# Batch norm constants, joins, third logits and a variance placed elsewhere in the first blocks of a codebook convolution

## The chip, the cores and the metric

One Trainium2 chip; the kernel runs on one of its cores. The time is the device time of one execution in microseconds. Before the change it is 2612.57 us, the median of three runs (2611.66 to 2615.24).

Engine names in the rows of the profile: PE is TensorE's matmul and PEld its weight load, DVE is VectorE, ACT is ScalarE, POOL is GpSimd, SP is SyncE, which issues most of the transfers here. A trailing q (SPq) is the issuing queue. L614 is line 614 of the kernel.

## The reference, cut to what matters

Two convolutions of 3x3, each computed with a codebook of 16 centroids per channel, around a group norm, two batch norms, a squeeze-and-excite gate and two residual additions. Input `x` is 16 x 256 x 28 x 28, float32.

```python
def amm_conv3x3(x, centroids, w_sub):          # centroids: C x 16 x 9
    p = patches of x                           # B x 784 x C x 9
    d = sum(p*p)[..., None] - 2 * einsum('bncs,cks->bnck', p, centroids) + sum(centroids*centroids)
    attn = softmax(-d, axis=-1)                # over the 16 centroids
    lut = einsum('cks,cso->cko', centroids, w_sub)
    return einsum('bnck,cko->bno', attn, lut)

def bn(x, gamma, beta, mean, var):
    inv = gamma * rsqrt(var + 1e-5)
    return x * inv + (beta - mean * inv)

g = group_norm(x, 32 groups)
h = relu(bn(amm_conv3x3(g, centroids1, wsub1), bn1))
y = bn(amm_conv3x3(h, centroids2, wsub2), bn2)
y = y * sigmoid(relu(mean(y) @ w1 + b1) @ w2 + b2)
out = x + relu(y + g)
```

## The kernel before

The work is cut into 128 blocks: two layers, 16 images, and in each image four blocks, one for each half of the channels (`hh`) and of the rows (`t`), in the order of `BLOCKS`: (0,0), (0,1), (1,1), (1,0). A block works on 128 channels and 14 x 28 = 392 positions. Its steps are:

- **Patches.** Each of the two patch tiles `pt` holds nine shifted copies of the input. For image 0 they come straight from a prepared input (`raw`, L269 to L273), with GpSimd or Vector adding the group norm's border terms (`border`, L510 to L530). From image 1 on, the normalised image is written to memory twice (`to_home1`) and read back by six transfers (`patches`, L585 to L595).
- **Logits** (`logits`, L605 to L619): four groups `mm` = 0 to 3, each of 16 small matmuls into two PSUM banks of two halves. ScalarE takes the exponentials (`exps`, L622 to L626).
- **Denominators** (`num_b`, L673 to L684) from all four exponentials, into one double bank `nb`. ScalarE copies it twice with different masks (`split_r`, L687 to L689, and `split_q`, L697 to L699); Vector adds the other half to each (`join_r`, L691 to L695, and `join_q`, L702 to L704), takes the reciprocal (`recip_dve`, L706) and spreads it over the channels by shuffles (`spread`, L715 to L723).
- **Numerators** (`num_a`, L659 to L669), four double banks `na`; each is multiplied by the reciprocal on Vector (`scale_a`, L737 to L741) or copied by ScalarE and multiplied on GpSimd (`copy_a`, `scale_q`).
- **Products** (`product`, L745 to L752): 128x128 matmuls with the lookup table. Four blocks need only seven products for two row halves and two channel halves each, since GpSimd forms differences of the blocks' inputs (`mix`, L754 to L758) and Vector adds results (`acc_add`, L783 to L790).

For image 0 the group norm is not applied to the image but folded into the weights: `raw_stats`, `raw_mean`, `raw_dev`, `raw_var`, `raw_norm` find mean and deviation, `mean_off` (L384 to L392) subtracts a mean from the weights, `tap_sum` (a matmul, L394), `tap_scale` and `tap_shift` (L401 to L411) scale them into `wx`. All this is done for each half of the weights (`h` = 0, 1; half 0 serves the logits 0 and 1, half 1 the logits 2 and 3). `later` and `later_tap` do the same for the second channel half. The statistics of image 1 (`gn_stats`, `gn_mean`, `gn_var`, `gn_apply`, L419 to L576) are taken in the usual way during blocks 2 and 3.

**What sets the order.** Each engine does its instructions in the order in which the program issues them. That order is written by hand: `at(cl, sub, f, ...)` files a job under a step `cl` and a position `sub`, and at the end the jobs run in the order of these two keys (L1541 to L1543), jobs with equal keys in the order in which they were filed. A block takes two steps. `TURN` moves a few logits of the first blocks to other keys.

**PSUM.** There are four double banks, numbered 0 to 3, and everything uses them in turn. In the first four blocks `EARLY` says which logits, numerators, denominators, product and small matmul takes which number; a matmul that wants a bank waits until its last reader has finished. `("lg", 1): ((1, 2), ...)` means that block 1's logits 0 take bank 1 for their first half and bank 2 for the second.

**Constants.** `vecs` holds the batch norms' parameters. `setup_bn` (L319 to L324) files two inverse square roots of `var` on GpSimd at (6, 2.75); `setup_shift` (L326 to L332) files the sign change of a bias (L327) and six small products and differences on Vector at (9, 2.1).

Of the kernel before, what the change touches and what calls it, by code (L numbers as in the profile page):

```python
# [30 lines left out]
BN_EPS = 1e-5  # L31
# [21 lines left out]
EARLY = {  # L53
# [4 lines left out]
    "acc": {4: 0, 6: 1, 7: 3}, "small": {4: 1},  # L58
}
TURN = {(2, 2): (4, 0.9), (2, 3): (4, 1.035), (3, 0): (5, 1.27), (3, 1): (5, 1.32), (3, 2): (7, 1.3), (3, 3): (7, 1.35)}  # L60
LAST = {0: (12, 2.05), 1: (8, 2.05), 2: (10, 2.05), 3: (11, 2.9)}
# [27 lines left out]
def kernel(  # L89
# [219 lines left out]
    def rsqrt(dst, src, eps, n):  # L309
        t = small.tile([P, n], F32, name="rs_t")  # L310
        nc.gpsimd.tensor_scalar(t, src, eps, None, op0=ALU.add)
        nc.gpsimd.tensor_tensor(dst, t, mhalf[:, :n], ALU.pow)
# [5 lines left out]

    def setup_bn():  # L319
        for l in range(2):  # L320
            sc = const.tile([P, NB], F32, name=f"bnsc{l}")
            sh = const.tile([P, NB], F32, name=f"bnsh{l}")
            rsqrt(sc, vecs[:, :, 4 * l + 3], BN_EPS, NB)
            bn.append((sc, sh))  # L324

    def setup_shift():  # L326
        nc.vector.tensor_scalar_mul(nb2_sb, vecs[:, :, 8], -1.0)  # L327
        for l, (sc, sh) in enumerate(bn):
            ga, be, mu = (vecs[:, :, 4 * l + i] for i in range(3))
            nc.vector.tensor_mul(sc, sc, ga)  # L330
            nc.vector.tensor_mul(sh, mu, sc)
            nc.vector.tensor_sub(sh, be, sh)  # L332

    cst = const.tile([P, 64], F32, name="cst")
# [145 lines left out]
    def raw_scales(ps):  # L480
        rr, rstd = raws["rr", 0], nrm[:, 0, 1, 0:1]
        nc.gpsimd.tensor_scalar(rr[:, 0], hot_sb[:, :16], rstd, None, op0=ALU.mult)
        nc.tensor.matmul(ps[:, 16:32], lhsT=eighth, rhs=rr[:, 0], start=True, stop=True)
        sq_add(0, 1)
        scm, ms = piece(16), piece(16)
        nc.vector.tensor_scalar(scm, ps[:, 16:32], hot_sb[:, 26:27], hot_sb[:, 27:28], op0=ALU.mult, op1=ALU.add)
        nc.vector.tensor_tensor(ms, ps[:, 16:32], raws["m2", 0], ALU.mult)
        raws["scm", 0], raws["ms", 0] = scm, ms
# [762 lines left out]
    for j, u in enumerate(blocks):  # L1251
# [26 lines left out]
        at(g, 1.05, split_r, u)  # L1278
        at(g, 1.2, join_r, u)
        at(g, 1.25, recip_dve, u)  # L1280
        at(g, 1.3 if j > 1 else 1.06, split_q, u)
        at(g, 1.35 if j > 1 else 1.21, join_q, u)
        g = 2 * j + 2 + (j > 1)
        for i, mm in enumerate(SLOT_MM):
            at(g, 1.0 + 0.01 * i, num_a, u, mm)
            if mm in kept:
                at(g, 1.05, copy_a, u, mm)
            else:
                if j == 1:
                    at(4, 0.835 if i else 0.815, spread, u, mm)  # L1290
                else:
                    at(g - 1, 2.05 if i == 4 - len(kept) and j > 1 else 1.4 + 0.01 * i, spread, u, mm)
                at(g, 1.04 + 0.001 * i, scale_a, u, mm)
# [7 lines left out]
    for l in range(2):  # L1301
        for b in range(B):
# [75 lines left out]
            if l == 0:  # L1378
# [8 lines left out]
                if b + 1 < B:  # L1387
                    at(*((g - 2 + (b == 1), 2.6 - (b == 1)) if b else (1, 1.6)), load_x, b + 1)
                    for q in range(NB):
                        at(*(((g + 1, 1.5) if b == 1 else (g, 0.3)) if b else (3, 1.3)), gn_stats, b + 1, q)  # L1390
                    at(*((g + 1, 2.1) if b else (4, 0.825)), gn_mean, b + 1, step=g + 1 if b else 4)
                    at(*((g + 3, 2.1) if b else (4, 0.845)), gn_var, b + 1, step=g + 3 if b else 4)
                    for q in range(NB):
                        at(*((g + 4, 1.9) if b else (4, (0.95, 1.055)[q])), gn_apply, b + 1, q)
                        at(*((g + 4, 1.92) if b else (4 + 3 * q, 1.6 + 0.05 * q)), to_home1, b + 1, q)
            else:
# [33 lines left out]
    for o in range(2):  # L1430
        at(11 + o, 0.5 if o else 1.9, code_spread, o)
    at(8, 0.6, code_load)
    at(14, 0.7, rank_row)
# [62 lines left out]
    raw_scales(ps)  # L1496
    tap_sum(0, 0, bank("tap", tag=0)[:, :256])
    tap_scale(0, 0)
    tap_shift(0, 0)
    at(-0.4, 0.5, mean_off, 0, 256, 512)  # L1500
    at(-0.4, 0.55, tap_scale, 0, 1)
    at(0, 0.15, lambda: tap_sum(0, 1, bank("tap", tag=3)[:, :256]))
    at(0, 0.2, tap_shift, 0, 1)
    for t in xpads:
# [27 lines left out]
    at(1, 1.44, tap_scale, 1, 0, 16, nc.gpsimd)  # L1532
    at(3, 0.9, later_tap)
    for h in range(2):
        at(3, 0.91, tap_shift, 1, h)
    at(6, 2.75, setup_bn)
    at(9, 2.1, setup_shift)
    for t in hpads:
# [184 lines left out]
```

## Time and profile before

| | us |
|---|---|
| median of three runs | 2612.57 (2611.66 to 2615.24) |
| the profiled execution | 2611.61 |
| its span, first to last instruction | 2610.1 |
| TensorE busy | 2589.5 (99%) |
| Vector busy | 1778.1 (68%) |
| ScalarE busy | 1372.3 (53%) |
| GpSimd busy | 1905.7 (73%) |
| mean clock granted to TensorE | 0.999 |

A busy time counts an engine from the start of an instruction to its end; matmuls are pipelined, so a TensorE that is busy isn't always at its peak. In a row of the timeline stand the start, the duration, the engine, the line, the operation, what it writes and reads, and the count; in brackets the engine's idle time ahead of it and what ended that. In a row of waits stand who waited, for whom, the sum of the waits, their number and the longest. In a row of windows stand the stretch, its length, each engine's busy time with its count of instructions, the clock granted to TensorE as a share of the full one, and what the transfer engines did.

### The profile page before, as it was taken

The page shows a single profiled execution, that of the slowest core. Times are in us where ns is not written, and L with a number is a line of the kernel's source. Part 1 is how long each engine was busy: PE and PEld are TensorE (multiplying, and loading weights), DVE is VectorE, ACT ScalarE, POOL GpSimd, SP SyncE. Part 2 cuts the span into 40 slices and gives each one's busy share as a digit, 9 for nine tenths or more (in the row PEclk, how much of TensorE's full clock was granted, in tenths as well). Part 3 has the DMA queues.
Part 4 walks back from the last instruction along what each step waited for, and adds up shares of the span by engine and source line. Part 5 has one row for each costly group of instructions (what it writes and reads, how often), then busy time and mean ns, then how long its engine had stood idle before and what let it go on. Part 6 is the DMA issues. An engine that isn't in the chain of part 4 may idle for free.

```text
span 2610.1 us, 85834 instructions
## 1 busy us (share of the span) xinstructions
PE 2589.5 (99%) x37026; PEld 1269.1 (49%) x37026; DVE 1778.1 (68%) x3797; ACT 1372.3 (53%) x1913; POOL 1905.7 (73%) x1341
## 2 busy tenths in 40 slices
PE   8999999999999999999999999999999999999999
PEld 3444444444444444444444444444444444444445
DVE  7776656666566666566676766767776667767676
ACT  6444444444444454444455655565555655555565
POOL 6786666866568766677666887778878788787786
PEclk9999999999999999999999999999999999999999
DMA  6556656555555576554664344444444444444432
GB/s 217 147 150 183 202 155 186 165 169 167 159 145 146 167 185 178 168 159 137 180 170 105 104 118 122 124 115 119 104 128 125 119 116 110 115 126 127 116 105 66
DMA packets 213289, 372.07 MB, mean 143 GB/s; under 512 B 29497, under 2 KB 183529, under 8 KB 212329
## 3 DMA queue, kind: packets, MB, share of 16 engines
q1 hardware_dynamic: 206584, 333.75, 46.9%
q0 software_dynamic: 6176, 32.66, 3.5%
q8 instruction: 295, 4.83, 0.8%
q14 instruction: 90, 0.73, 0.1%
q10 hardware_dynamic: 144, 0.10, 0.0%
HBM read 288.46 MB, written 77.95 MB: 140 GB/s over the span
## 4 chain that ended last, share of the span: by engine, by line
PE 98%; DVE 1%; ACT 0%; POOL 0%; issue 0%; DMA 0%; SPq 0%; POOLq 0%; ACTq 0%
PE acc L749 52%; PE lg L614 17%; PE na L665 14%; PE nb L679 14%; ACT e L625 0%; PE sep L1050 0%; DVE rb L722 0%; POOL qp L758 0%; PE tap L395 0%; PE sep L1042 0%; DVE nb_sb L327 0%; DMA xt<-in_x 0%; PE sqp L377 0%; PE sqp L346 0%; POOL qp L730 0%
## 5 line engine op out<-in xcount | busy, mean ns | idle before, releaser
L749 PE MATMUL acc<-qp,wall 128*128 128x392 f32 (+1 forms) x3088 | 1099.3, 499 | 0.3 <-POOL qp L758 0.2
L625 ACT ACTIVATE e<-lg 128x784 f32<-128x784 f32 x960 | 737.8, 821 | 637.2 <-PE lg L614 634.2
L758 POOL TENSOR_TENSOR qp<-qp,qp 128x784 f32<-128x784 f32 x512 | 944.6, 1869 | 151.3 <-DVE qp L741 150.8
L749 PEld LDWEIGHTS acc<-qp,wall 128*128 128x128 f32 x3088 | 568.0, 190 | 505.9 <-issue 54.6
L722 DVE STREAM_SHUFFLE rb<-r 128x392 f32<-128x392 f32 x1024 | 550.8, 604 | 0.0
L614 PE MATMUL lg<-pt,wd 32*32 32x392 f32 x15872 | 468.9, 499 | 2.9 <-DVE hpad L786 2.0
L693 DVE SCALAR_TENSOR_TENSOR r<-nb,kst,r 128x392 f32<-128x392 f32 x128 | 80.1, 626 | 444.7 <-ACT r L689 442.3
L665 PE MATMUL na<-e,cwa 64*32 64x392 f32 x8192 | 374.5, 492 | 1.4 <-DVE gn_var L562 1.4
L741 DVE TENSOR_TENSOR qp<-na,rb 128x784 f32<-128x784 f32 x352 | 333.9, 972 | 60.8 <-PE na L665 49.8
L679 PE MATMUL nb<-e,cwb 64*32 64x392 f32 x8192 | 373.8, 492 | 0.1
L730 POOL TENSOR_TENSOR qo<-qo,rb 128x392 f32<-128x392 f32 x128 | 131.3, 1026 | 295.3 <-DVE rb L718 294.6
L707 DVE RECIPROCAL r<-r 128x392 f32<-128x392 f32 x128 | 333.2, 2603 | 4.4
L730 POOL TENSOR_TENSOR qp<-qp,rb 128x784 f32<-128x784 f32 x160 | 295.7, 1858 | 2.9
L679 PEld LDWEIGHTS nb<-e,cwb 64*32 64x32 f32 x8192 | 189.0, 106 | 175.5 <-issue 21.8
L665 PEld LDWEIGHTS na<-e,cwa 64*32 64x32 f32 x8192 | 182.0, 106 | 184.9 <-issue 75.1
L614 PEld LDWEIGHTS lg<-pt,wd 32*32 32x32 f32 x15872 | 116.1, 103 | 269.6 <-issue 235.5
L749 PE MATMUL acc<-qp,w_A 128*128 128x392 f32 x512 | 182.4, 499 | 0.0
L689 ACT ACTIVATE r<-nb,kst 128x392 f32<-128x392 f32 x128 | 86.8, 678 | 165.9 <-PE nb L679 162.8
L649 POOL TENSOR_TENSOR z<-z,mx 128x1568 f32<-128x1568 f32 x32 | 91.8, 2869 | 94.6 <-DVE mx L643 94.6
L749 PE MATMUL acc<-qo,wall 128*128 128x392 f32 (+1 forms) x386 | 157.9, 491 | 0.0
L735 ACT COPY qp<-na 128x784 f32<-128x784 f32 x160 | 130.0, 813 | 22.4 <-PE na L665 20.6
L749 PEld LDWEIGHTS acc<-qp,w_A 128*128 128x128 f32 x512 | 94.6, 190 | 82.5 <-DVE qp L741 19.8
(241 smaller groups left out, 1707.3 us busy)
## 6 DMA issues: line engine op xcount, KB each, us to landing
pt<-home SPq DMA_DIRECT2D x744, 209.0 KB
pt<-home SPq DMA_DIRECT2D x744, 104.5 KB
home<-xpad SPq DMA_DIRECT2D x30, 899.0 KB
xt<-in_x SPq DMA_DIRECT2D x30, 784.0 KB
out_dram<-y SPq DMA_DIRECT2D x31, 392.0 KB
pt<-in_p SPq DMA_DIRECT2D x6, 784.0 KB
d_wS<-st SPq DMA_DIRECT2D x12, 192.0 KB
wall<-d_wS SPq DMA_DIRECT2D x4, 576.0 KB
```

The lines of the kernel that those rows point to most:

```text
L614: nc.tensor.matmul(bk[32 * c : 32 * c + 32, :N].rearrange("p (r w) -> p r w", w=W), lhsT=(wx[u["hh"]] if early(u) else wts["wd", u["hh"]]) ...
L625: nc.scalar.activation(eg[:, 2 * i : 2 * i + 2, :], bk[:, :, :N], AF.Exp, scale=2.0)
L649: nc.gpsimd.tensor_tensor(zk, zk, mx.unsqueeze(2).to_broadcast([P, N // 4, K]), ALU.subtract)
L665: nc.tensor.matmul(bs[32 * i : 32 * i + 32, r, :N], lhsT=wts["cwa", u["hh"]][64 * r : 64 * r + 64, mm, i, :], rhs=es[64 * r : 64 * r + 64, ...
L679: nc.tensor.matmul(bs[32 * i : 32 * i + 32, r, :N], lhsT=wts["cwb", u["hh"]][64 * r : 64 * r + 64, mm, i, :], rhs=es[64 * r : 64 * r + 64, ...
L707: nc.vector.reciprocal(u["r"], u["r"])
L722: nc.vector.stream_shuffle(rb[:, r, :], u["r"], mask_of(2 * mm + r))
L730: nc.gpsimd.tensor_tensor(q, q, u.pop(("rb", mm)), ALU.mult)
L735: nc.scalar.copy(pair(u, mm), u.pop(("na", mm))[:, :, :N])
L741: nc.vector.tensor_mul(pair(u, mm), u.pop(("na", mm))[:, :, :N], rb)
L749: nc.tensor.matmul(accs[key][:, : cols[1] - cols[0]], lhsT=wl[w][:, k, :], rhs=us["q", k][:, cols[0] : cols[1]], start=first and n == 0, s ...
L758: nc.gpsimd.tensor_tensor(pair(out_u, mm), pair(in0, mm), pair(in1, mm), ALU.subtract)
```

## The change

In the order of the diff:

- block 0's numerators, and some logits of blocks 1 and 2, get other PSUM banks; block 1's third logits (`mm` = 2) move from step 3 to (2, 0.9), ahead of block 0's numerators at (2, 1.0);
- `setup_shift` is merged into `setup_bn`, and the whole moves to (1, 0.47), behind the second half's squares on Vector;
- the scale and shift of image 0's group norm (`scm`, `ms`) become a function of their own, `raw_scm`; the second half's `mean_off` moves ahead of it, and its tap sum ahead of the first logits, its tap scale and shift to (-0.4, 0.5) and (-0.4, 0.6);
- for blocks 0 and 1, `join_r` moves from 1.2 to 1.055, right behind `split_r`; `split_q` and `join_q` move into the next step, (g + 1, 0.12) and 0.13; block 0's first spreads move behind them, to (2, 0.14);
- two of block 1's spreads move from 0.835 to 0.847, behind `gn_var` at 0.845;
- `gn_stats` of image 1 moves from (3, 1.3) to (4, 0.14); `load_x` of image 2 from (7, 1.6) to (8, 1.6), the second `to_home1` of image 1 from (7, 1.65) to (8, 1.55), `code_load` from (8, 0.6) to (8, 1.65); `later_tap` from (3, 0.9) to (2, 1.9).

```diff
-    ("lg", 0): ((0, 1), (2, 3), (0, 1), (2, 3)), ("nb", 0): 0, ("na", 0): (0, 2, 3, 1),
-    ("lg", 1): ((1, 2), (3, 1), (2, 1), (0, 3)), ("nb", 1): 2, ("na", 1): (1, 0, 3, 2),
-    ("lg", 2): ((1, 0), (3, 2), (3, 2), (1, 0)), ("nb", 2): 3, ("na", 2): (0, 2, 3, 1),
+    ("lg", 0): ((0, 1), (2, 3), (0, 1), (2, 3)), ("nb", 0): 0, ("na", 0): (1, 0, 2, 3),
+    ("lg", 1): ((1, 2), (3, 1), (2, 3), (0, 3)), ("nb", 1): 2, ("na", 1): (1, 0, 3, 2),
+    ("lg", 2): ((1, 0), (3, 1), (3, 2), (1, 0)), ("nb", 2): 3, ("na", 2): (0, 2, 3, 1),
...
-TURN = {(2, 2): (4, 0.9), (2, 3): (4, 1.035), (3, 0): (5, 1.27), (3, 1): (5, 1.32), (3, 2): (7, 1.3), (3, 3): (7, 1.35)}
+TURN = {(1, 2): (2, 0.9), (2, 2): (4, 0.9), (2, 3): (4, 1.035), (3, 0): (5, 1.27), (3, 1): (5, 1.32), (3, 2): (7, 1.3), (3, 3): (7, 1.35)}
...
     def setup_bn():
+        nc.vector.tensor_scalar_mul(nb2_sb, vecs[:, :, 8], -1.0)
         for l in range(2):
+            ga, be, mu, va = (vecs[:, :, 4 * l + i] for i in range(4))
             sc = const.tile([P, NB], F32, name=f"bnsc{l}")
             sh = const.tile([P, NB], F32, name=f"bnsh{l}")
-            rsqrt(sc, vecs[:, :, 4 * l + 3], BN_EPS, NB)
-            bn.append((sc, sh))
-
-    def setup_shift():
-        nc.vector.tensor_scalar_mul(nb2_sb, vecs[:, :, 8], -1.0)
-        for l, (sc, sh) in enumerate(bn):
-            ga, be, mu = (vecs[:, :, 4 * l + i] for i in range(3))
+            rsqrt(sc, va, BN_EPS, NB)
             nc.vector.tensor_mul(sc, sc, ga)
             nc.vector.tensor_mul(sh, mu, sc)
             nc.vector.tensor_sub(sh, be, sh)
+            bn.append((sc, sh))
...
         nc.tensor.matmul(ps[:, 16:32], lhsT=eighth, rhs=rr[:, 0], start=True, stop=True)
         sq_add(0, 1)
+
+    def raw_scm(ps):
         scm, ms = piece(16), piece(16)
...
-        at(g, 1.2, join_r, u)
+        at(g, 1.2 if j > 1 else 1.055, join_r, u)
         at(g, 1.25, recip_dve, u)
-        at(g, 1.3 if j > 1 else 1.06, split_q, u)
-        at(g, 1.35 if j > 1 else 1.21, join_q, u)
+        at(*((g, 1.3) if j > 1 else (g + 1, 0.12)), split_q, u)
+        at(*((g, 1.35) if j > 1 else (g + 1, 0.13)), join_q, u)
...
-                    at(4, 0.835 if i else 0.815, spread, u, mm)
+                    at(4, (0.815, 0.835, 0.847, 0.847)[i], spread, u, mm)
                 else:
-                    at(g - 1, 2.05 if i == 4 - len(kept) and j > 1 else 1.4 + 0.01 * i, spread, u, mm)
+                    at(*((g - 1, 2.05 if i == 4 - len(kept) and j > 1 else 1.4 + 0.01 * i) if j else (2, 0.14)), spread, u, mm)
...
-                    at(*((g - 2 + (b == 1), 2.6 - (b == 1)) if b else (1, 1.6)), load_x, b + 1)
+                    at(*(((8, 1.6) if b == 1 else (g - 2, 2.6)) if b else (1, 1.6)), load_x, b + 1)
                     for q in range(NB):
-                        at(*(((g + 1, 1.5) if b == 1 else (g, 0.3)) if b else (3, 1.3)), gn_stats, b + 1, q)
+                        at(*(((g + 1, 1.5) if b == 1 else (g, 0.3)) if b else (4, 0.14)), gn_stats, b + 1, q)
...
-                        at(*((g + 4, 1.92) if b else (4 + 3 * q, 1.6 + 0.05 * q)), to_home1, b + 1, q)
+                        at(*((g + 4, 1.92) if b else (4 + 4 * q, 1.6 - 0.05 * q)), to_home1, b + 1, q)
...
-    at(8, 0.6, code_load)
+    at(8, 1.65, code_load)
...
     raw_scales(ps)
-    tap_sum(0, 0, bank("tap", tag=0)[:, :256])
-    tap_scale(0, 0)
+
+    def first_half():
+        raw_scm(ps)
+        tap_sum(0, 0, bank("tap", tag=0)[:, :256])
+        tap_scale(0, 0)
+
+    mean_off(0, 256, 512, first_half)
+    tap_sum(0, 1, bank("tap", tag=3)[:, :256])
     tap_shift(0, 0)
-    at(-0.4, 0.5, mean_off, 0, 256, 512)
-    at(-0.4, 0.55, tap_scale, 0, 1)
-    at(0, 0.15, lambda: tap_sum(0, 1, bank("tap", tag=3)[:, :256]))
-    at(0, 0.2, tap_shift, 0, 1)
+    at(-0.4, 0.5, tap_scale, 0, 1)
+    at(-0.4, 0.6, tap_shift, 0, 1)
...
-    at(3, 0.9, later_tap)
+    at(2, 1.9, later_tap)
     for h in range(2):
         at(3, 0.91, tap_shift, 1, h)
-    at(6, 2.75, setup_bn)
-    at(9, 2.1, setup_shift)
+    at(1, 0.47, setup_bn)
```

`mean_off` calls the function that it is given between its sum and its subtraction.

## The prediction

> **What bounds the kernel now.** I read the page first: TensorE is busy for 99% of the span, so a change can pay only where TensorE stands still or runs slowly. The second view is that of the waits of TensorE over the whole span; these are the four of its rows that the change touches:
>
> ```profile
> PE 2589.5 (99%) x37026; PEld 1269.1 (49%) x37026; DVE 1778.1 (68%) x3797; ACT 1372.3 (53%) x1913; POOL 1905.7 (73%) x1341
> ...
> PE lg L614 <- DVE pt L520: 2.0, 1, 2.0
> PE lg L614 <- DVE hpad L786: 2.0, 1, 2.0
> PE na L665 <- DVE gn_var L562: 1.4, 1, 1.4
> PE lg L614 <- DVE qo L704: 1.0, 1, 1.0
> ```
>
> They sum to 6.4 us of 2610.1. The largest other wait is that of the first matmul for its data; the rest are pieces of 0.6 us or less. So the gain has a ceiling near 6.4 us, plus the slowness that the stalls bring with them and the time in which matmuls are drawn out by late PSUM banks. The first of these is in the third view, the windows of 2 us behind the stall that ends at 99.26, with the TensorE timeline there:
>
> ```profile
> 99.26 0.95 PE L614 MATMUL lg<-pt,wd 32*32 32x392 f32 x32 [1.98 <-DVE hpad L786]
> ...
> 100.00:102.00 2.00, 2.00 (x19) 1.08 (x4) 2.00 (x1) 1.70 (x3) 2.00 (x2) 0.57 0.13 22
> 102.00:104.00 2.00, 2.00 (x5) 1.07 (x4) 1.85 (x8) 0.41 (x1) 2.00 (x2) 0.58 0.80 236
> ```
>
> The granted clock, the third number from the end, is 0.57 and 0.58 right behind the stall, and 1.00 in the windows on both sides. That loses 0.43 and 0.42 of 2 us each: the stall costs its 1.98 us and 1.7 us more.
>
> I call the blocks u0 to u7 in their order, and cut the working into four places.
>
> **Place 1, around 97 us (constants of the batch norm): 3.7 us.** The Vector and GpSimd timelines show what the 1.98 us are:
>
> ```profile
> 94.12 3.13 DVE L327 TENSOR_SCALAR nb_sb<-vecs 128x2 f32<-128x2 f32 x1
> ...
> 98.08 1.03 DVE L786 TENSOR_TENSOR hpad<-acc,hpad 128x392 f32<-128x392 f32 x2
> ...
> 94.36 1.03 POOL L730 TENSOR_TENSOR qo<-qo,rb 128x392 f32<-128x392 f32 x1
> 95.35 1.87 POOL L730 TENSOR_TENSOR qp<-qp,rb 128x784 f32<-128x784 f32 x1
> ```
>
> L327 handles two elements per partition and takes 3.13 us: it ends at 97.25, when GpSimd's unbroken run ends at 97.22. With six small operations behind it, the add L786 that frees the PSUM bank of u5's second logits starts at 98.08. The change takes all seven away from here. L786 can then start at about 94.2 and end at 95.2. TensorE, whose wait began at 99.26 - 1.98 = 97.28, finds the bank free: 1.98 + 1.7 = 3.7 us. Next late would be GpSimd's sums behind L786, but they come earlier too, by as much as its two scalings allow.
>
> The Trainium skill, "SBUF — State Buffer", section "SBUF: two separate sides", says that GpSimd and a Vector operation in a two-port mode hold a shared port pair as an exclusive lock for a whole instruction; L327's end 0.03 us behind GpSimd's agrees. By that rule L327 can be held wherever it is put; what that would do here is part of the second rival.
>
> The constants go behind (1, 0.45). These rows count there:
>
> ```profile
> 16.54 0.25 POOL L530 TENSOR_TENSOR pt<-pt,first 128x16 f32<-128x16 f32 x1
> ...
> 21.89 0.94 POOL L517 TENSOR_TENSOR wall<-wall,first 128x208 f32<-128x208 f32 x1 [2.89 <-DMA wall<-in_p]
> ...
> 66.75 0.22 POOL L311 TENSOR_SCALAR rs_t<-vecs 128x2 f32<-128x2 f32 x1
> ...
> 68.06 0.71 POOL L312 TENSOR_TENSOR bnsc<-rs_t,mhalf 128x2 f32<-128x2 f32 x1
> ...
> 22.38 0.16 DVE L446 TENSOR_TENSOR first<-sqp,gn_mv 128x1 f32<-128x1 f32 x1 [3.46 <-PE sqp L377]
> ```
>
> The four GpSimd instructions run from 66.75 to 68.77, 2.0 us. GpSimd waits for a transfer from 19.0 to 21.89, so they fit at 19.0 to 21.0. Vector's seven end at 21.7 to 22.2, the later figure if L327 waits until GpSimd pauses. Behind them in Vector's line stands L446, the start of `raw_dev`, which has 3.46 us of idle time ahead of it and ran at 22.38. So the seven are covered, unless place 2 brings L446 forward by more than 0.2 to 0.7 us; I count 0.1 lost. GpSimd's 2.0 us around 67 only deepen the slack of the mixes there.
>
> **Place 2, before 25 us (the first logits): 0.6 us.** TensorE, then one row each of Vector and GpSimd:
>
> ```profile
> 12.95 1.62 PE L614 MATMUL lg<-pt,first 32*32 32x392 f32 x32 [1.98 <-DVE pt L520]
> ...
> 15.66 4.57 PE L614 MATMUL lg<-pt,first 32*32 32x392 f32 x96
> 20.76 0.38 PE L439 MATMUL sqp<-gn_mv,gmat 128*128 128x2 f32 x2 [0.54 <-ACT e L625]
> ...
> 11.01 0.43 DVE L410 TENSOR_TENSOR tap<-tap,first 128x256 f32<-128x256 f32 x1 [0.28 <-PE tap L395]
> ...
> 15.15 0.94 POOL L517 TENSOR_TENSOR pt<-pt,first 128x208 f32<-128x208 f32 x1 [5.88 <-DMA wall<-in_p]
> ```
>
> The 1.98 us ahead of the first logits do not go. Their border (L520) stays behind L410, and L410 is bound by TensorE's tap sum; the second half's subtraction, about as long as L410, mostly fills the gap of 0.28 us ahead of it. What goes is the second tap sum, 1.1 us between the first logits' end (14.57) and the second's start (15.66): it now runs inside that stall. So u0's second logits run from 14.6 to 16.2. The third wait for GpSimd's border, which a transfer holds until 15.15 and which ends with L530 at 16.8; no edit touches that. They run from 16.85 to 18.5 (1.62 us as the first), two exponentials of 0.74 us follow (row 26.60 below), and the bank that L439 needs is free at 20.0 instead of 20.7. Of these 0.7 us I keep 0.6.
>
> **Place 3, 25 to 42 us (order of block 1, joins): 1.7 us more.** TensorE, ScalarE, Vector:
>
> ```profile
> 28.31 3.75 PE L665 MATMUL na<-e,cwa 64*32 64x392 f32 x64
> ...
> 36.06 2.86 PE L679 MATMUL nb<-e,cwb 64*32 64x392 f32 x64
> ...
> 42.46 4.22 PE L749 MATMUL acc<-qp,w_A 128*128 128x392 f32 x12
> ...
> 26.60 2.97 ACT L625 ACTIVATE e<-lg 128x784 f32<-128x784 f32 x4
> ...
> 26.57 0.62 DVE L693 SCALAR_TENSOR_TENSOR r<-nb,kst,r 128x392 f32<-128x392 f32 x1 [0.49 <-ACT qo L699]
> ...
> 38.04 0.42 DVE L411 TENSOR_TENSOR first<-tap,first 128x256 f32<-128x256 f32 x1
> ...
> 40.32 0.63 DVE L693 SCALAR_TENSOR_TENSOR r<-nb,kst,r 128x392 f32<-128x392 f32 x1 [1.85 <-ACT qo L699]
> ```
>
> The join L693 waits for the second copy L699, which it does not read. Behind its own copy it starts about 1.1 us earlier for u0 and 2.1 for u1, and the reciprocal with it. The second join now waits for a copy that lies behind two exponentials, and u0's spreads stand behind that join, so I step through. u1's exponentials, at 26.60 before, go at 26.0 and 26.7; then the copy; then 28.0 and 28.7. They end at 29.55 as before (26.60 + 2.97), since the copy stands among them. So u0's numerators start later, at 29.6 instead of 28.3, and end at 32.5 instead of 32.06. But u1's third logits are done by then, inside 27.6 to 29.8, while TensorE would wait for banks. Behind the numerators come only the tap sum (1.1), the fourth logits (0.95) and u1's denominators, at 34.5 instead of 36.1: 1.6 us. Vector is the next bound: five spreads and four tap operations, 0.5 us each, from 33.0, end at 37.4 (before 38.46), and u2's first logits need that bank. They run from 37.45 to 38.4. The second ones no longer use the bank that the second join frees, which removes the wait of 1.0 us. The first product starts at 40.2 against 42.5: 2.3 us gained in all.
>
> **Place 4, 42 to 60 us (variance between the shuffles): 1.0 us more.**
>
> ```profile
> 51.23 2.87 PE L665 MATMUL na<-e,cwa 64*32 64x392 f32 x64 [1.37 <-DVE gn_var L562]
> ...
> 55.02 2.87 PE L679 MATMUL nb<-e,cwb 64*32 64x392 f32 x64
> ...
> 48.02 0.60 DVE L722 STREAM_SHUFFLE rb<-r 128x392 f32<-128x392 f32 x1
> ...
> 51.01 0.16 DVE L562 TENSOR_TENSOR gn_var<-gn_gm,gnp 128x2 f32<-128x2 f32 x1
> 52.22 3.62 DVE L741 TENSOR_TENSOR qp<-na,rb 128x784 f32<-128x784 f32 x4 [1.05 <-PE na L665]
> ```
>
> Six shuffles lay between the means and L562, from 48.02 to 51.01, 0.5 us each. Now two lie there, and L562 comes at 46.8, right behind its own matmul: the 1.37 us go. The four shuffles behind it end at 48.9, the four scalings (0.9 each) at 52.5, and u2's denominators need the bank of the third: 51.7 instead of 55.02. So 0.3 us come back as waits for scalings, and the gain there is 3.3 us. The statistics that moved behind the second join end at about 44.0, ahead of their matmul at 45.1: hidden.
>
> From 60 to 97 us TensorE has no wait in which to spend the lead, and hands it on whole if SP's queue holds:
>
> ```profile
> 71.95 3.87 SPq L592 DMA_DIRECT2D pt<-home  x6
> 75.92 0.38 SPq L186 DMA_DIRECT2D xt<-in_x  x1
> ...
> 79.99 3.54 SPq L592 DMA_DIRECT2D pt<-home  x5
> ...
> SPq L592 <- DMA xt<-in_x: 0.2, 1, 0.2
> ...
> 89.06 1.02 DVE L427 BATCH_NORM_STATS2 gn_st<-xt 128x6 f32<-128x392 f32 x2
> ...
> 93.28 0.28 PE L535 MATMUL gnp<-gn_mv,gmat 128*128 128x4 f32 x2
> ```
>
> Image 2, the second padded write and the codes go behind u5's six patch transfers, which can issue from about 76.5 on and take 3.9 us like u4's. The image then issues near 80.9 instead of 75.92, on the clock of before. A patch transfer between 79.99 and 83.5 waited for its end, so it landed near 83, 7 us after its issue; now near 88, ahead of 89.06. Two pairs of statistics take 2.4 us, to 91.5, and their matmul comes at 93.28: 1.8 us more of slack. No cost.
>
> **Sum.** 0.6 + 1.7 + 1.0 + 3.7 = 7.0 us. The profiled execution took 2611.61 us (span 2610.1 and 1.5 around it): 2604.6. The median of the runs shown, 2612.57, is 0.96 above it; I go between and forecast 2605.0.
>
> **Rivals.**
> *The slow clock comes anyway.* TensorE could lose a stretch to half clock elsewhere, as between 26 and 30 us, where u1's logits wait for banks. For it: such waits stay. Against it: those of 1.0 and 1.4 us show none. Price 1.7: 2606.3. The Trainium skill, "TensorE: Matmul & The Clock Gate", section "What's actually happening", wants a whole idle window of about 3.4 us before half clock, in windows that run free of the kernel. By that the gap of 1.98 us would not be the cause, and the loss could stay. The trace speaks against it, as the slow stretch begins within 1 us of the gap's end.
> *The lead is lost in blocks 0 and 1.* u1's third logits stand in TensorE's line ahead of u0's numerators: if their border comes late, everything behind waits. L327, if it is held until GpSimd's border is done at 23.7, delays u0's variance matmul in the same way, by 2.5 us. Then places 2 and 3 give nothing: 3.7 + 1.0 leaves 2606.9.
> *The image comes late: the other side.* The matmul at 93.28 stands in TensorE's line. A landing later than 91 costs us for us, and a stall of 2 us brings the slow clock, 1.7. A landing near 96.2, 15 us after its issue, eats all 7 us by a stall of 5.3 and the clock; at 17 us the kernel takes about 2613.3. Measured now are 7 us.
>
> **Chances.** Forecast (2603 to 2606.2) 0.56; clock 0.12; lead lost, to 2608, 0.20; late image 0.08, half of it beyond 2613; better than 2603, 0.04. A difference under 0.2%, 5.2 us, is about what cannot be told from no change. Against the median 2612.57 that line is at 2607.4: forecast, clock, better and a few of the lead lost make faster 0.75; same 0.20; slower 0.05. The range from 2602.5 to 2609.0 takes in the first three cases.
>
> **What will show it.** Right: no wait of L614 for L786 near 90 and a clock of 1.00 behind it; the first product at 40 to 40.5 and u2's denominators near 51.7; the wait ahead of the first logits still 2 us; no wait of TensorE at the means of image 2. Wrong: a new wait at u1's third logits, a stretch at half clock anywhere, or the statistics of image 2 released by a transfer.

## The result, and the profile after

The changed kernel takes 2605.85 us, the median of 11 runs (2604.14 to 2608.67); the kernel before, on the same chip, takes 2612.66 (11 runs, 2610.59 to 2615.49). The ratio is 0.9975 (95% interval 0.9967 to 0.9983), or 6.8 us less (4.4 to 8.6). The forecast was 2605.0. The profiled execution of the changed kernel took 2607.78 us, so it is one of the longer ones: only one of the eleven took longer.

All line numbers of TensorE's and Vector's work are smaller by one to three in the changed kernel (the logits L614 are L613, the adds L786 are L785). First the page's row of busy time, then the waits of TensorE over the whole span:

```profile
PE 2591.2 (99%) x37026; PEld 1273.2 (49%) x37026; DVE 1776.6 (68%) x3797; ACT 1371.7 (53%) x1913; POOL 1905.6 (73%) x1341
```

```profile
PE flp L1219 <- DVE fl L1215: 0.7, 1, 0.7
PE lg L613 <- PE tap L392: 0.6, 1, 0.6
```

The four rows that the prediction began with, 6.4 us together, are gone: what is left behind the first data is 0.7 us or less in one piece. One of the four was forecast to stay, the 1.98 us ahead of the first logits. These start no earlier (13.11 us, 12.95 before); the second half's tap sum now fills the stall, as the prediction's own working has it, and what is left is a wait of 0.6 us for that sum. So a row that goes doesn't say where the time came from, and a wait that goes may come back as matmuls that are drawn out. For this, compare starts on TensorE's timeline. The changed kernel:

```profile
13.11 5.92 PE L613 MATMUL lg<-pt,first 32*32 32x392 f32 x128 [0.62 <-PE tap L392]
...
20.97 2.86 PE L678 MATMUL nb<-e,cwb 64*32 64x392 f32 x64
...
41.16 4.22 PE L748 MATMUL acc<-qp,w_A 128*128 128x392 f32 x12
```

Its first product starts at 41.16, though 40.2 was forecast. The windows of 2 us show why; the third number from the end is the granted clock:

```profile
28.00:30.00 2.00, 1.82 (x24) 0.41 (x32) 2.00 (x9) 2.00 (x4) 1.89 (x2) 0.64 1.04 402
30.00:32.00 2.00, 2.00 (x36) 0.94 (x27) 1.83 (x4) 0.35 (x1) 1.92 (x5) 0.51 0.80 277
```

This is the stretch at half clock of the first rival, in the very place that it named: 0.36 + 0.49 of 2 us each, 1.70 us. So this profile shows the forecast case and the rival mixed, and one profile can't take them apart. The experiments begin there.

### The profile page after: what moved, and what is told of

The parts are those of the page before. It is cut to its first block, busy times and chain, and to the rows that moved or that the text cites. A ratio compares the mean times of both kernels' runs of the same rounds, so it can differ in the third digit from the quotient of the medians.

```text
span 2606.2 us, 85832 instructions
## 1 busy us (share of the span) xinstructions
PE 2591.2 (99%) x37026; PEld 1273.2 (49%) x37026; DVE 1776.6 (68%) x3797; ACT 1371.7 (53%) x1913; POOL 1905.6 (73%) x1341
## 4 chain that ended last, share of the span: by engine, by line
PE 99%; ACT 0%; POOL 0%; DVE 0%; issue 0%; DMA 0%; POOLq 0%; ACTq 0%
PE acc L748 52%; PE lg L613 17%; PE na L664 14%; PE nb L678 14%; ACT e L624 0%; PE sep L1049 0%; POOL qp L757 0%; PE sep L1041 0%; DMA xt<-in_x 0%; PE tap L392 0%; PE sqp L374 0%; PE sqp L343 0%; POOL qp L729 0%; PE gnp L534 0%; PE gnp L551 0%
## 5 line engine op out<-in xcount | busy, mean ns | idle before, releaser
L613 PE MATMUL lg<-pt,wd 32*32 32x392 f32 x15872 | 469.0, 499 | 0.2
L613 PEld LDWEIGHTS lg<-pt,wd 32*32 32x32 f32 x15872 | 116.4, 103 | 266.6 <-issue 238.3
```

The costliest lines, as they stand in the source:

```text
L613: nc.tensor.matmul(bk[32 * c : 32 * c + 32, :N].rearrange("p (r w) -> p r w", w=W), lhsT=(wx[u["hh"]] if early(u) else wts["wd", u["hh"]]) ...
```

## The experiments

There were twelve more: ten kernels, and each of the two once more. Times are medians; the ratio is to the kernel before on the same chip. The chips differ (the kernel before takes 2611.03 to 2612.66 us on them), so compare ratios, not times.

| kernel | time, us | ratio (95%) | slow stretch in its profile, up to 120 us |
|---|---|---|---|
| before again | 2612.70, one run | | 100 to 104 |
| changed again | 2603.67, one run | | none |
| sign early | 2610.88 | 0.9998 (0.9989 to 1.0007) | 42 to 48 |
| constants early | 2608.95 | 0.9991 (0.9982 to 1.0) | none |
| constants late | 2607.88 | 0.9987 (0.9978 to 0.9996) | 32 to 38, 100 to 106 |
| constants behind | 2615.70 | 1.0015 (1.0006 to 1.0024) | 108 to 114 |
| variance between | 2610.24, one run | | none |
| block 1 only | 2613.84, one run | | 30 to 36 |
| prologue old | 2606.32, one run | | none |
| queue old | 2605.14, one run | | none |
| image late | 2615.08 | 1.0016 (1.0006 to 1.0025) | 94 to 102 |
| tried further | 2605.62 | 0.9973 (0.9964 to 0.9983) | none |

### Both kernels once more

> The kernel before, once more, for a second trace. The changed kernel's trace leads by 6.3 us at 120 us and by 4.1 at the end. If the 2.2 us between are the change's doing, this trace keeps the times of the first one from 120 us to the end within 0.5 us. If they are the scatter of single executions, it drifts against the first by a like amount, 1 to 3 us, in small pieces at other places.

> The changed kernel, once more. Its first trace has half clock from 28.6 to 32.0 and u1's denominators at 35.4, where 34.5 was forecast. If the slow stretch belongs to the order of block 1, it is here again at about the same place and the first product is at 41.2. If it depends on where the clock's windows fall, it is elsewhere or missing, and then the first product is at 40.0 to 40.4.

The kernel before had its slow stretch at 100 us again. The changed kernel had none at all, and so it shows the change by itself. TensorE's timeline in this second profile of the changed kernel:

```profile
13.25 5.66 PE L613 MATMUL lg<-pt,first 32*32 32x392 f32 x128 [0.61 <-PE tap L392]
...
20.98 2.86 PE L678 MATMUL nb<-e,cwb 64*32 64x392 f32 x64
...
34.41 2.92 PE L678 MATMUL nb<-e,cwb 64*32 64x392 f32 x64
...
40.26 4.22 PE L748 MATMUL acc<-qp,w_A 128*128 128x392 f32 x12
...
51.72 2.87 PE L678 MATMUL nb<-e,cwb 64*32 64x392 f32 x64
...
93.78 0.94 PE L613 MATMUL lg<-pt,wd 32*32 32x392 f32 x32
```

Forecast were 34.5, 40.2 and 51.7 for u1's denominators, the first product and u2's denominators. Executions begin up to 0.3 us apart, so I compare distances. The kernel before has the same points at 12.95, 22.27 (u0's denominators, the row below), 42.46, 55.02 and 99.26:

```profile
22.27 2.86 PE L679 MATMUL nb<-e,cwb 64*32 64x392 f32 x64
```

First logits to u0's denominators: 9.32 before, 7.73 after, 1.59 gained. From there to the first product: 20.19 and 19.28, 0.91. To u2's denominators: 12.56 and 11.46, 1.10. To u5's second logits: 44.24 and 42.06, 2.18. That is 5.78 us. Behind this point the kernel before lost another 1.7 to its slow clock.

### The sign change alone, early

```diff
 # in setup_shift
-        nc.vector.tensor_scalar_mul(nb2_sb, vecs[:, :, 8], -1.0)
 # where the constants are placed
+    at(1, 0.47, lambda: nc.vector.tensor_scalar_mul(nb2_sb, vecs[:, :, 8], -1.0))
```

> The kernel before with one Vector instruction moved, the sign change of two elements that took 3.13 us at 94.12: it goes to (1, 0.47), the six small products stay at (9, 2.1). If that one instruction, held until GpSimd pauses, is the cause at 97 us, the add that frees the bank starts at about 95 (six products of 0.15 us), ends before 96, the wait of 1.98 us and the half clock behind it go, and the kernel gains 3.7 us: 2608.9. If the six products or a wait for GpSimd's roots are the cause, the wait stays near 2 us and the time at 2612.6. If the slow clock is no consequence of the wait, the gain is 2.0 us: 2610.6.

No gain: 0.9998 (on this chip the kernel before takes 2611.03, so that 2610.88 isn't the third case). Vector's timeline around 97 us in this kernel, then GpSimd's:

```profile
96.16 3.10 DVE L329 TENSOR_TENSOR bnsc<-bnsc,vecs 128x2 f32<-128x2 f32 x1
```

```profile
97.31 1.94 POOL L729 TENSOR_TENSOR qp<-qp,rb 128x784 f32<-128x784 f32 x1
100.67 1.98 POOL L792 TENSOR_TENSOR hpad<-hpad,half_sum 128x392 f32<-128x392 f32 x2 [1.43 <-DVE hpad L785]
```

With L327 gone, the next operation in line takes the hold: 3.10 us for two elements, until GpSimd pauses at 99.25. So nothing is special about the sign change. TensorE's wait stays 1.77 us. The Trainium skill, "SBUF — State Buffer", section "SBUF: two separate sides", says that the lock also binds a Vector operation with two SBUF inputs, against a GpSimd operation that reads SBUF. L329 is one, and its row agrees that it is held.

See also why GpSimd pauses at all. The second row's bracket says that its next operation waited for the adds L785, which stand in Vector's line *behind* the six that are left there. The hold ends because GpSimd in its turn waits for what is held up.

### All seven constants, behind the adds

```diff
-    at(9, 2.1, setup_shift)
+    at(10, 0.02, setup_shift)
```

> The kernel before with one move: all seven constants behind the two adds of L786 instead of ahead of them, still in the middle of GpSimd's unbroken run. Theory that the place in Vector's line is what cost the time: the first of the seven is held as before until GpSimd pauses near 97.2 us and takes some 2 us, but L786 starts near 94.2 instead of 98.1, TensorE does not wait for it at 97 to 99 us, and the waits of TensorE lose their row of 2.0 us; the slow clock behind it goes too if it hung on that wait. That is 2.0 us without the clock (about 2610.6, ratio 0.9992) and 3.7 with it (about 2608.9, ratio 0.9986). Rival, that the hold costs the same wherever it lies in that stretch: the join behind the seven comes late instead, and TensorE waits 1 to 2 us for its bank; ratio 1.000.

The wait that the prediction is about goes, as the first theory said (TensorE's second logits of u5 start at 97.50). But the kernel is slower, by more than the rival's price. Vector's timeline, then GpSimd's, then the row of TensorE:

```profile
94.41 1.03 DVE L786 TENSOR_TENSOR hpad<-acc,hpad 128x392 f32<-128x392 f32 x2
95.35 3.09 DVE L327 TENSOR_SCALAR nb_sb<-vecs 128x2 f32<-128x2 f32 x1
...
99.50 1.77 DVE L332 TENSOR_TENSOR bnsh<-vecs,bnsh 128x2 f32<-128x2 f32 x1
...
104.79 0.61 DVE L693 SCALAR_TENSOR_TENSOR r<-nb,kst,r 128x392 f32<-128x392 f32 x1
```

```profile
97.46 1.99 POOL L793 TENSOR_TENSOR hpad<-hpad,half_sum 128x392 f32<-128x392 f32 x2
99.40 5.45 POOL L758 TENSOR_TENSOR qp<-qp,qp 128x784 f32<-128x784 f32 x3
```

```profile
108.59 1.19 PE L614 MATMUL lg<-pt,wd 32*32 32x392 f32 x32 [4.03 <-issue]
```

GpSimd has its sums early now and doesn't pause: L793 at 97.46 has no wait in its row, and three mixes follow without a gap. So five of the seven are held, one after the other, each until a GpSimd instruction ends, and the seven take 9.5 us where they took 4.0. The join L693 behind them starts at 104.79 instead of 99.03, and TensorE stands still for 4.03 us. The price of a small Vector operation here isn't its own: it is set by the GpSimd instructions that run beside it, as long as GpSimd has work.

### The constants early, by themselves, and taken out of the change

```diff
 # constants early: the kernel before, with setup_bn of the change
-    at(6, 2.75, setup_bn)
-    at(9, 2.1, setup_shift)
+    at(1, 0.47, setup_bn)
 # constants late: the changed kernel, with the opposite edit
```

> The kernel before with all constants at the early place and nothing else of the change. Theory of the prediction: place 1 by itself is worth 2.0 us of wait, up to 3.7 with the slow clock in runs that had it there: ratio 0.9986 to 0.9992, L786 near 94.2, GpSimd at L793 from 97.3 instead of 98.7, and no wait of TensorE for L786. It costs 0.1 us or less ahead of 25 us. Rival one, that another held operation takes the place of the constants, as when L327 alone was moved: the wait for L786 stays above 1.5 us and the ratio is 1.000. Rival two, that the constants hold up L446 at 22.4 us: the second half of block 0's logits and all behind it come 0.5 us or more later.

> The changed kernel with the batch norm's constants where they were: roots on GpSimd at (6, 2.75), sign change and six products on Vector at (9, 2.1). If place 1 is worth 3.7 us on its own, the time goes back to 2605.9 + 3.7 = 2609.6, with the wait of 2 us for the add and a granted clock near 0.57 behind it. If the lead of the first blocks covers the held instruction, less than 2 us come back: under 2608.

By itself the early place is worth 0.0009 in the ratio, about 2.4 us of 2611 (0 to 4.7); the medians differ by 2.1. Without it the changed kernel is at 0.9987 instead of 0.9975; the difference is some 3 us, with intervals as wide. The expectation's bounds of 2608 and 2609.6 can't be used as they stand, since this chip's kernel before is 1.6 us faster than the one that they were worked out from: by 2607.88 alone the second case would hold, and by the ratio the place is worth about 3 us, between the two. In the timeline of the kernel with early constants the adds start at 94.69, GpSimd's sums have no wait, and TensorE runs through (first row, GpSimd; second, TensorE); with late ones the wait is back (third):

```profile
96.47 1.99 POOL L790 TENSOR_TENSOR hpad<-hpad,half_sum 128x392 f32<-128x392 f32 x2
```

```profile
97.78 0.94 PE L611 MATMUL lg<-pt,wd 32*32 32x392 f32 x32
```

```profile
100.75 1.21 PE L616 MATMUL lg<-pt,wd 32*32 32x392 f32 x32 [1.95 <-DVE hpad L788]
```

That settles the 2.0 us of wait. It doesn't give the 3.7 that the prediction put on this place, to which 1.7 of slow clock were added. The next two kernels bear on that.

### The variance alone, and block 1's order alone

```diff
 # variance between
-                    at(4, 0.835 if i else 0.815, spread, u, mm)
+                    at(4, (0.815, 0.835, 0.847, 0.847)[i], spread, u, mm)
 # block 1 only: from the change, the lines of EARLY and TURN, join_r, split_q and join_q,
 # u0's spreads, gn_stats of image 1 and later_tap
```

> The kernel before with the variance of image 1 between its shuffles and nothing else of the change. Theory: the wait of 1.37 us for L562 at 51 us goes, and with it some 0.3 us come back as a wait for scalings, so that the denominators of block 2 start near 54.0 instead of 55.0 and the lead stays at 1.0 us up to 97 us. Rival, that the four shuffles behind it are late instead: the scalings start later than 52.2 and the denominators of block 2 wait for them, 55.0 as before.

> The kernel before with the order of block 1, the joins, block 0's spreads and the tap operations of half 2 as changed, without the edits ahead of 25 us, the constants and the variance. Theory: the first product starts 1.7 us earlier than in the kernel before (41.3 from 43.0), and the wait of 1.0 us for the join of the second denominators (L704) goes. The wait for L562 stays, so block 2's denominators are 1.7 to 2.3 us early. Rival, that this order gains only when the first logits come early too: under 0.7 us at the first product, with a new wait of TensorE near 29 us ahead of block 0's numerators. A stretch at half clock between 25 and 40 us would take 1.7 us off either.

TensorE's timeline with the variance alone:

```profile
54.04 2.87 PE L679 MATMUL nb<-e,cwb 64*32 64x392 f32 x64
...
98.29 0.95 PE L614 MATMUL lg<-pt,wd 32*32 32x392 f32 x32 [1.95 <-DVE hpad L786]
...
99.18 4.22 PE L749 MATMUL acc<-qp,wall 128*128 128x392 f32 x12
```

54.04 was forecast as 54.0. Look at the last two rows: here is the wait of 2 us at full length, and the twelve products behind it take 4.22 us, their time at full clock. The wait doesn't always bring the slow stretch.

Block 1's order alone went the other way. Its windows, and its first product:

```profile
30.00:32.00 2.00, 2.00 (x40) 0.74 (x48) 2.00 (x9) 2.00 (x3) 1.88 (x5) 0.76 0.87 218
32.00:34.00 2.00, 2.00 (x40) 0.84 (x32) 1.20 (x2) 0.51 (x2) 1.83 (x5) 0.50 0.43 163
34.00:36.00 2.00, 2.00 (x35) 0.93 (x20) 1.21 (x3) 0.90 (x2) 0.60 (x2) 0.89 0.06 24
```

```profile
43.02 4.22 PE L749 MATMUL acc<-qp,w_A 128*128 128x392 f32 x12
```

0.48 + 1.00 + 0.22 are again 1.70 us. Without them the first product would start between 41.3 and 42.0 (in the changed kernel such a stretch moved it by 1.0, from 27.01 to 28.05 us behind the first logits). The first theory said 41.3, the rival's bound is 42.3, and the rival's wait ahead of block 0's numerators isn't there. But both bounds start from 43.0, the second profile of the kernel before; from the first logits the gain without the stretch would be 0.7 to 1.8 us, against either profile of that kernel (28.1 to 28.8 us instead of 29.5 and 30.0). This run leans to the theory and doesn't decide, because the clock took the gain away.

### The order ahead of the first logits, and SP's order, as before

> The changed kernel with the order of the tap sums ahead of the first logits as before. Theory of the prediction: block 0's denominators start 0.6 to 1.3 us later than 21.0, and all behind them by as much, since TensorE has no idle time between: block 1's denominators at 35.0 to 35.7 where the changed kernel without a slow stretch has them at 34.4, first product at 40.9 to 41.6. Rival, that the exponentials and joins of 24 to 34 us bound it: denominators of block 0 late, first product at 40.3 to 40.5 all the same. A stretch at half clock between 25 and 40 us would add 1.7.

> The changed kernel with the load of image 2, the second padded write and the codes at their old places in SP's line. Theory of the prediction: no cost and no gain either way: the image issues near 73 us, Vector's statistics of it stay near 86.7, TensorE has no wait of over 0.5 us between 60 and 100 us, and the second logits of block 5 stand near 93.8 plus what slow stretches cost ahead of it. Rival, that the new order is what keeps the lead: block 5's patches are late behind those transfers, and TensorE waits for a transfer of 0.5 us or more between 80 and 100.

The edits are those of the diff, undone. With the old prologue TensorE shows:

```profile
21.84 2.86 PE L676 MATMUL nb<-e,cwb 64*32 64x392 f32 x64
...
41.29 4.22 PE L746 MATMUL acc<-qp,w_A 128*128 128x392 f32 x12
```

Both lie in the first theory's intervals, 0.86 and 1.03 us behind the second profile of the changed kernel; so the prologue's lead is handed on as far as the first product. It is a low measure of that lead. (This run's start was a fast one: its last 96 first logits took 3.90 us, where the same order took 4.57 in the profile before.)

With SP's old order the image issues at 72.73 (first row, SP's queue), and TensorE keeps the lead (second):

```profile
72.73 0.38 SPq L186 DMA_DIRECT2D xt<-in_x  x1
```

```profile
94.06 0.94 PE L613 MATMUL lg<-pt,wd 32*32 32x392 f32 x32
```

Against 12.95 and 99.26 before, with first logits at 13.10 here, that is 5.35 us; 5.78 with the new order, in one run each, and neither has a wait of TensorE between 60 and 100 us. The order of these transfers is worth nothing that these runs can tell.

### The image later still

```diff
-                    at(*(((8, 1.6) if b == 1 else (g - 2, 2.6)) if b else (1, 1.6)), load_x, b + 1)
+                    at(*(((9, 1.5) if b == 1 else (g - 2, 2.6)) if b else (1, 1.6)), load_x, b + 1)
```

> The changed kernel with the load of image 2 moved once more, behind block 5's second six patch transfers, so that it issues near 88.9 us instead of 78.7. Theory, the price of the prediction's rival on the other side: with 7 us to land it is there near 96, the statistics end near 98.5, and TensorE waits about 7.5 us at the means of image 2, with a slow stretch behind it: 2613 to 2615, ratio 1.0003 to 1.001. Rival, that a transfer with fewer others beside it lands in 4 us: statistics end near 95.3, a wait of 4.5 us, 2610 to 2612, ratio 0.999 to 0.9998.

2615.08, at the edge of the first theory's times; the ratio, 1.0016, is above its 1.0003 to 1.001, and the theory's times leave out that the kernel before is faster on this chip (2611.05). SP's issue, Vector's statistics, TensorE's matmul of the means, and the clock:

```profile
88.93 0.39 SPq L186 DMA_DIRECT2D xt<-in_x  x1
```

```profile
95.22 1.04 DVE L424 BATCH_NORM_STATS2 gn_st<-xt 128x6 f32<-128x392 f32 x2 [8.79 <-DMA xt<-in_x]
```

```profile
97.79 0.56 PE L534 MATMUL gnp<-gn_mv,gmat 128*128 128x4 f32 x2 [7.21 <-DVE gn_mv L425]
```

```profile
94.00:96.00 2.00, 0.00 (x0) 0.00 (x0) 0.78 (x2) 0.00 (x0) 0.00 (x0) 0.76 0.06 25
96.00:98.00 2.00, 0.21 (x2) 0.24 (x2) 1.57 (x5) 0.00 (x0) 0.00 (x0) 0.50 0.00 0
98.00:100.00 2.00, 2.00 (x42) 0.72 (x50) 1.52 (x6) 0.06 (x1) 0.45 (x1) 0.50 0.00 0
100.00:102.00 2.00, 2.00 (x32) 0.84 (x33) 0.00 (x0) 1.48 (x2) 1.92 (x3) 0.54 0.00 0
```

Vector takes up the image 6.3 us after its issue. TensorE waits 7.2 us and then runs slowly to 102. The clock is halved for two stretches of 3.4 us (0.48 + 1.00 + 1.00 + 0.92 = 3.40, twice 1.70), but TensorE stands still in the first 2.8 us of them, so that some 2.0 us are lost to it. So the rival on the other side was real, with its price. The issue here is 10.2 us later than the changed kernel's at 78.70, and 7.2 us of that came back as a wait: some 3 us of slack (an estimate from these two) kept the rival away.

### One step further

```diff
 # only for block 0: copy and join of the second denominators, and three of four spreads, later
-        at(*((g, 1.3) if j > 1 else (g + 1, 0.12)), split_q, u)
+        at(*((g, 1.3) if j > 1 else (g + 1, 0.12 if j else 0.315)), split_q, u)
-        at(*((g, 1.35) if j > 1 else (g + 1, 0.13)), join_q, u)
+        at(*((g, 1.35) if j > 1 else (g + 1, 0.13 if j else 0.32)), join_q, u)
-                    at(*((g - 1, 2.05 if i == 4 - len(kept) and j > 1 else 1.4 + 0.01 * i) if j else (2, 0.14)), spread, u, mm)
+                    at(*((g - 1, 2.05 if i == 4 - len(kept) and j > 1 else 1.4 + 0.01 * i) if j else (2, 0.33 if i else 0.14)), spread, u, mm)
```

> The changed kernel with the copy of block 0's second denominators, its join and three of its four spreads moved behind the exponentials of block 1 that block 0's numerators wait for. Theory that in 24 to 42 us ScalarE's line sets the time: the numerators of block 0 start 0.6 to 0.9 us earlier than 29.4, the denominators of block 1 and the first product as much earlier, and the whole takes 0.6 to 1.5 us less than the changed kernel (2604.4 to 2605.3; ratio to before 0.9969 to 0.9972). Rival, that Vector's spreads bound the first product: the numerators come earlier, the first product does not (41.2 as in the changed kernel's profile, 40.3 without its slow clock), and the time is that of the changed kernel (ratio 0.9975).

```profile
28.40 0.89 PE L664 MATMUL na<-e,cwa 64*32 64x392 f32 x16
30.07 2.40 PE L664 MATMUL na<-e,cwa 64*32 64x392 f32 x48 [0.78 <-DVE qo L703]
...
40.07 4.22 PE L748 MATMUL acc<-qp,w_A 128*128 128x392 f32 x12
```

The numerators start at 28.40, 0.6 us earlier than in the second profile of the changed kernel. Three quarters of them then wait 0.78 us for the bank that the later join frees. The first product comes at 40.07, against 40.26; from the first logits that is 26.98 against 27.01. The time is that of the changed kernel, as the rival said, though a bank held the numerators and not the spreads.

## Why the prediction was right

**Place 1, 3.7 us forecast, about 2.2 found: the mechanism right, the clock wrongly put to it.** The wait was 1.98, and 2.18 us are gained there by the starts; the early constants alone gave 2.1 by the medians. The 1.7 us of slow clock were tied to this wait because the stretch began within 1 us of its end. That step failed: it took one coincidence for a price that is always paid. In the profiles with the wait of 1.6 to 2.0 us, the stretch came behind it three times of six (before, before again, constants late), and three times not (sign early, block 1 only, variance between). And every run lists its mean clock: a stretch costs 1.70 of 2610 us and leaves at most 0.9993, so a run that reads 1.000 had none. Of 61 runs of the kernel before, beside the experiments, 30 read 1.000, all with the same wait in their program. Without it there are still 0.999s: 5 of 11 runs of the changed kernel, 4 of 11 with the constants early. (The 0.999s count too many, as variance between shows, with 0.999 and no stretch ahead of the last 10 us.) What the change takes from the clock is then some tenths of a us in the mean (an estimate from these counts), not 1.7.

Here the prediction weighed a rule of the Trainium skill against the trace and sided with the trace. "TensorE: Matmul & The Clock Gate", section "What's actually happening", says that the clock is set by windows of about 3.4 us that run free of the kernel, so that the same program differs by run. The runs agree: every stretch takes 1.70 us from the clock or twice that, 3.4 us at half clock, and it comes or stays away in one and the same kernel. The same section of the Trainium skill gives half clock to a whole idle window. The changed kernel's profile shows otherwise: its stretch begins at 28.6 us, and in the 10 us ahead TensorE's longest wait is 0.43 us. There the measurement decides: half clock can come without an idle window.

The traces tell a part of when it comes. With late constants the two stretches begin at 33.05 and 101.31 us, 20 steps of 3.413 us apart, so I count such steps from a stretch in each trace (with the variance alone, from the one in its last 4 us). In the step that holds most of the wait at 97 us TensorE is busy for 1.4, 1.4 and 1.5 us in the three profiles with the stretch behind it (before, before again, constants late), and for 1.6, 2.0 and 2.4 us in the three without. Two of these rows, the kernel before and the variance alone:

```profile
96.87:100.28 3.41, 1.43 (x46) 0.41 (x34) 3.24 (x12) 0.68 (x1) 1.83 (x3) 1.00 0.02 5
```

```profile
96.85:100.26 3.41, 1.97 (x35) 0.95 (x36) 3.34 (x7) 1.14 (x3) 2.43 (x3) 1.00 0.03 5
```

The steps lie differently in every execution. So the wait seems to bring the stretch only where it leaves TensorE little enough to do within one step, and that it did so in the profile before was the luck of that execution. Six cases show an order and no threshold, and busy time isn't all of it: in the step ahead of the changed kernel's stretch TensorE was busy for 3.0 of 3.4 us. What counts stays open.

**That the constants cost nothing in the new place: right.** Vector's timeline in the changed kernel:

```profile
17.42 0.35 DVE L320 TENSOR_SCALAR nb_sb<-vecs 128x2 f32<-128x2 f32 x1
...
20.76 0.16 DVE L328 TENSOR_TENSOR bnsh<-vecs,bnsh 128x2 f32<-128x2 f32 x1
21.08 0.16 DVE L443 TENSOR_TENSOR first<-sqp,gn_mv 128x1 f32<-128x1 f32 x1 [0.16 <-PE sqp L374]
```

The prediction put them into GpSimd's wait for a transfer. They came earlier, while GpSimd clears two tiles (its row below) and then does six short operations of 0.2 to 0.7 us:

```profile
16.08 1.64 POOL L1545 MEMSET xpad<- 128x900 f32 x2
```

The sign change takes 0.35 us there and not 3.1, and the six behind it 0.16 each: with nothing long on GpSimd, there is no long hold. The seven end 0.16 us ahead of the next operation's data. The second rival, in which the hold moves along, didn't come.

**Place 2, 0.6 forecast, 1.5 found.** From the first logits to u0's denominators the order before takes 9.32 us (9.32 with the variance alone, 8.65 with the old prologue), the new one 7.73 to 8.00 in five of six profiles. The term that was mis-sized is ScalarE's. The prediction put two exponentials behind the whole of the third logits. But each exponential needs only one half of them, 16 matmuls, so the first of the two runs beside the second half. ScalarE's timeline shows it, in the kernel before and in the changed one:

```profile
17.32 0.82 ACT L625 ACTIVATE e<-lg 128x784 f32<-128x784 f32 x1 [1.18 <-PE lg L614]
18.45 3.69 ACT L625 ACTIVATE e<-lg 128x784 f32<-128x784 f32 x5 [0.31 <-PE lg L614]
```

```profile
14.77 6.08 ACT L624 ACTIVATE e<-lg 128x784 f32<-128x784 f32 x8 [2.46 <-PE lg L613]
```

The eight exponentials now run in one piece, and the 1.18 + 0.31 us for which ScalarE waited for logits are the 1.5 us gained. The border, for which the prediction held the third logits until 16.8, isn't the cause. With the image later still, GpSimd started it at 15.24, later than the 15.15 that the prediction read; the third logits waited, and u0's denominators still came 7.81 us behind the first logits:

```profile
16.95 1.99 PE L613 MATMUL lg<-pt,first 32*32 32x392 f32 x64 [0.41 <-POOL pt L529]
...
21.05 2.86 PE L678 MATMUL nb<-e,cwb 64*32 64x392 f32 x64
```

A border that is later than that can cost: it started between 13.85 and 15.62 in the profiles, and at 15.62, with late constants, the third logits waited 0.83 us, ScalarE 1.08, and u0's denominators came 10.24 us behind the first logits. In that execution, whose slow start also lasted longest (see the last section), the lead of this place was lost.

**Place 3, 1.7 forecast, 0.9 found.** 20.19 us from u0's denominators to the first product became 19.28 (19.45 with the old prologue). From the first logits to the first product the two errors cancel: 2.3 were forecast for both places, 2.50 came, and the starts that were forecast (34.5, 40.2) were met within 0.1 us.

**Place 4, 1.0 forecast, 1.1 found**, in the changed kernel and alone. **SP's order, no cost: right.**

**The sum.** 7.0 forecast; 5.8 by the starts, 6.8 (4.4 to 8.6) by the medians. It held because two terms that were too large, the clock and place 3, met one that was too small; that is luck, since the errors have separate causes. The 1.0 us between the two measures is partly the clock's tenths; the rest lies behind 112 us, where the lead over the first profile moves in pieces of 0.2 to 1.4 us from run to run: the changed kernel loses 2.2 us of it in its first profile and gains 1.0 in its second, and the kernel before loses 0.4 in its second. No edit touches that part. What moves it was not tried.

## What to carry to other kernels

A tiny Vector operation is not cheap beside unbroken long work on GpSimd; put it where GpSimd has only short work or none, not merely somewhere else in the line. Before a loss is counted to a wait because it stands behind it, look for the same wait without the loss in other runs; one profile can't tell a cause from a coincidence. Where one engine takes over another's work in halves, step the sum by halves: one term was off by 0.9 us, and an exponential of 0.7 us counted in line instead of beside the matmuls is most of that.

## What the runs showed of the hardware that was not expected

A Vector operation on two elements per partition took 3.09 to 3.13 us where it was the first of the seven in GpSimd's unbroken run, in all four profiles that show it (before, sign early, constants late, constants behind). It didn't get through at the first two ends of GpSimd instructions, only at the third. Those behind it took 0.15 us, or, where GpSimd went on, 0.93 to 1.77, until the next end.

The clock column doesn't show the slow start. It reads 1.00 from 0 to 20 us in the kernel before, while 32 logits take 1.62 us at 13 us and 0.95 at 99. The trace's own list of clock states begins only at 18.4 us there, at 16.5 to 20.8 in the others, and at 26.2 with late constants. When TensorE gets fast differs in the same way: the first denominators took 2.86 us in most profiles, and 4.22 in the one with late constants, where the third logits had waited 0.8 us; that execution was the slowest of its eleven, 2614.34 us.
